# An attention and feed-forward kernel: a fixed order on every engine, weighted sums one step later, band scores with alternating heads

## The chip, the cores and the metric

One core of a Trainium2 chip. The core has five engines with queues of their own: TensorE (PE; PEld is its weight load), VectorE (DVE), ScalarE (ACT), GpSimd (POOL) and SyncE (SP, which here only issues DMAs). The metric is the time of the program on the device, in microseconds; 4103.99 us is the median of three runs of the kernel before (4099.41 to 4113.84).

## The reference

The input x has the shape (2, 256, 128, 128): batch, time T, band FB, channel C. All numbers are 32-bit floats.

```
xt = _ln(x, ln_t_w, ln_t_b).transpose(0, 2, 1, 3)
x = x + _mha(xt, t_wi, t_bi, t_wo, t_bo, H_T, cm).transpose(0, 2, 1, 3)
xf = _ln(x, ln_f_w, ln_f_b)
x = x + _mha(xf, f_wi, f_bi, f_wo, f_bo, H_F, bm)
xn = _ln(x, ln_n_w, ln_n_b)
h = jax.nn.gelu(xn @ w1.T + b1, approximate=False)
x = x + (h @ w2.T + b2)
```

`_ln` normalizes over the channels. `_mha` is attention with four heads of 32 channels: first over the 256 times of each band with a causal mask `cm`, then over the 128 bands of each time with a mask `bm` that leaves the bands at a distance of at most 16. The feed-forward layer has 512 hidden channels.

## The kernel before

A check at the start (`fold`, which also folds the normalization's weights into the projections) picks the path without a row maximum; `BoundedPath` is the one that runs.

**Groups.** The work is cut into 384 groups of 4 tiles, each of 128 rows by 128 channels. The first 128 are `OverTime` groups (two bands with 256 times each); a time group reads x, and its result goes to a buffer x1 in device memory. Then come 32 blocks, each of four `OverBands` groups (four times with 128 bands each) and four `FeedForward` groups on the same 16 times. I call the first 128 groups the time phase and the rest the band phase.

**Steps of a group.** Mean and variance (tiles stats, mv; DVE) and the power -1/2 (rstd; POOL); normalized rows (xh; DVE); transposed on TensorE (xp) and copied (xnT; DVE). Then, for attention, products for queries, keys and values (qp, kp, vp; TensorE), taken out of PSUM as qT (ACT), kT and v (DVE). The scores sp (TensorE) are split in two halves, `first_half` and `second_half`: in the time phase one of the group's two bands, in the band phase two of the four heads. Their exponentials go to p (ACT; its tiles are named pt in the time phase and pf in the band phase), and POOL sets the masked ones to 0 with affine selects. `weigh` makes the weighted sums op and the row sums rp of the exponentials (TensorE), `invert` the logarithm ln and from it the reciprocal r0 (ACT), `divide` the products t and u and the quotient oT, a Newton step (DVE). `output` makes the last product yp (TensorE) and adds it to rd or x2, into which POOL's `bias` has put the input plus a row (DVE); in the time phase rd is then stored. A feed-forward group has hidden products hp (TensorE), gelus hT (ACT), the output product zp (TensorE), which is added to res (DVE), and a store.

**Which part of the array.** A head has 32 channels. The score products of a head use 32 rows of TensorE's array (32*128 in the profile), the products op and rp of a head 32 columns (128*32).

**What sets the order.** `run` (lines 804 to 830) goes through the groups; in step n it calls steps of the groups n - 1 to n + 5 in the order of its list. What it writes is a priority: a scheduler with a timeline of its own then moves instructions of each engine past each other where it expects an engine to wait. Only the order of table loads on ACT is tied (`exp_set`, `gelu_set`, `load_exp_set`): Exp and Ln need one table set, Gelu another. PSUM has 8 banks, which the products take in turn; a product waits until the readers of the bank's last tile are done. p, hT have 2 buffers, rd has 4, the x tiles 3.

Lines that the prediction speaks of: 446 to 451 statistics, 457 xh, 467 xp, 469 xnT, 498 bias, 510 to 526 projections, 532 ln, 534 r0, 540 to 544 division, 550 yp, 579 and 582 scores of the time phase, 586 and 589 their exponentials and masks, 620 and 622 row sums there, 642 scores of the band phase, 644 and 648 exponentials and masks there, 667 and 670 weighted sums and row sums there, 689 hp, 709 zp, 766 load of x.

Of the kernel before, what the change touches and what calls it, by code (L numbers as in the profile page):

```python
# [18 lines left out]
P = 128  # L19
# [404 lines left out]
class Group:  # L424
# [3 lines left out]

    def __init__(self, path, src, dst, before=None, store=None):
        self.path, self.src, self.dst = path, src, dst  # L430
        self.before, self.store = before, store
# [9 lines left out]
    def statistics(self):  # L441
        path, nc = self.path, self.path.nc
        self.mv = path.small.tile([P, NT, 2], F32, name="mv")
        stats = path.small.tile([P, NT, 6], F32, name="stats")
        for i in range(NT):
            nc.vector.bn_stats(stats[:, i, :], self.src()[:, i, :])
        for i in range(NT):
            nc.vector.bn_aggr(self.mv[:, i, :], stats[:, i, :])  # L448
        self.rstd = path.small.tile([P, NT], F32, name="rstd")
        nc.gpsimd.tensor_scalar(self.rstd, self.mv[:, :, 1], EPS, None, ALU.add)  # L450
        nc.gpsimd.tensor_tensor(self.rstd, self.rstd, path.k.mhalf, ALU.pow)  # L451

    def normalize(self):
        path, nc = self.path, self.path.nc
        self.xh = path.work.tile([P, NT, P], F32, name="xh")
        for i in range(NT):
            nc.vector.tensor_scalar(
# [4 lines left out]
    def transpose(self):  # L462

        path, nc = self.path, self.path.nc
        xp = path.bank([P, NT * P], "xp")
        for i in range(NT):
            nc.tensor.transpose(xp[:, i * P : (i + 1) * P], self.xh[:, i, :], path.k.ident)  # L467
        self.xnT = path.work.tile([P, NT * P], F32, name="xnT")
        nc.vector.tensor_copy(self.xnT, xp)  # L469

    def first_half(self):
        pass
# [4 lines left out]
    def second_half(self):  # L477
        pass
# [3 lines left out]

    def weigh(self):
        pass
# [6 lines left out]


class Attention(Group):
    which = None

    def bias(self):
        self.dst_tile()
        self.path.nc.gpsimd.tensor_tensor(  # L498
            self.dst(), self.src(),
            self.path.k.orow[self.which].unsqueeze(1).to_broadcast([P, NT, P]), ALU.add,  # L500
# [5 lines left out]
    def queries_keys(self):  # L506
        path, nc = self.path, self.path.nc
        wf = path.k.wf[self.which]
        qp = path.bank([P, NT * P], "qp")
        nc.tensor.matmul(qp, wf[:, 0:P], self.xnT, start=True, stop=True)  # L510
        self.qT = path.work.tile([P, NT * P], F32, name="qT")
        nc.scalar.activation(self.qT, qp, AF.Identity, bias=path.k.bq[self.which], scale=1.0)

        kp = path.bank([P, NT * P], "kp")
        nc.tensor.matmul(kp, wf[:, P : 2 * P], self.xnT, start=True, stop=True)  # L515
        self.kT = path.work.tile([P, NT * P], F32, name="kT")
        nc.vector.tensor_copy(self.kT, kp)

    def values(self):
        path, nc = self.path, self.path.nc  # L520
        wv = path.k.wf[self.which][:, 2 * P : 3 * P]
        vp = path.bank([P, NT, P], "vp")
        for i in range(NT):
            nc.tensor.matmul(vp[:, i], self.xnT[:, i * P : (i + 1) * P], wv, start=True, stop=True)  # L524
        self.v = path.work.tile([P, NT, P], F32, name="v")
        nc.vector.tensor_copy(self.v, vp)

    def invert(self):

        path, nc = self.path, self.path.nc  # L530
        ln = path.work.tile([P, NT * P], F32, name="ln", bufs=2)
        path.exp_set(nc.scalar.activation(ln, self.rp, AF.Ln))  # L532
        self.r0 = path.work.tile([P, NT * P], F32, name="r0", bufs=2)
        path.exp_set(nc.scalar.activation(self.r0, ln, AF.Exp, scale=-1.0))  # L534

    def divide(self):

        path, nc = self.path, self.path.nc
        t = path.work.tile([P, NT * P], F32, name="t", bufs=2)
        nc.vector.tensor_tensor(t, self.rp, self.r0, ALU.mult)  # L540
        u = path.work.tile([P, NT * P], F32, name="u", bufs=2)
        nc.vector.tensor_tensor(u, self.op, self.r0, ALU.mult)  # L542
        self.oT = path.work.tile([P, NT * P], F32, name="oT", bufs=2)
        nc.vector.scalar_tensor_tensor(self.oT, t, 2.0, u, ALU.subtract, ALU.mult)  # L544

    def output(self):
        path, nc = self.path, self.path.nc
        yp = path.bank([P, NT, P], "yp")
        for i in range(NT):
            nc.tensor.matmul(  # L550
                yp[:, i], self.oT[:, i * P : (i + 1) * P], path.k.wn[self.which], start=True, stop=True
            )
        nc.vector.tensor_tensor(self.dst(), yp, self.dst(), ALU.add)
# [8 lines left out]
class OverTime(Attention):  # L562
# [6 lines left out]
    def dst_tile(self):  # L569
        rd = self.path.work.tile([P, NT, P], F32, name="rd", bufs=4)  # L570
        self.dst = lambda: rd

    def scores(self, s):
        path, nc = self.path, self.path.nc
        W, a = self.W, 2 * s * P
        for h in range(H):
            r = rows_of(h)
            sp = path.bank([P, W], "sp")
            nc.tensor.matmul(
                sp[:, 0 : 2 * P], self.kT[r, a : a + P], self.qT[r, a : a + 2 * P], start=True, stop=True  # L580
            )
            nc.tensor.matmul(  # L582
                sp[:, 2 * P : W], self.kT[r, a + P : a + 2 * P], self.qT[r, a + P : a + 2 * P],
                start=True, stop=True,
            )
            path.exp_set(nc.scalar.activation(self.p[:, s, h, :], sp, AF.Exp))  # L586
        for n in (0, 2):
            blk = self.p[:, s, :, n * P : (n + 1) * P]
            nc.gpsimd.affine_select(  # L589
                out=blk, in_=blk, compare_op=ALU.is_ge, fill=0.0, base=0,  # L590
# [3 lines left out]
    def first_half(self):  # L594
        self.p = self.path.work.tile([P, 2, H, self.W], F32, name="pt", tag="p", bufs=2)
        self.scores(0)

    def second_half(self):
        self.scores(1)

    def weigh(self):
        path, nc = self.path, self.path.nc
        p, v, W = self.p, self.v, self.W
        op = path.bank([P, 2, 2 * P], "op")
        for s in range(2):
            for h in range(H):
                r = rows_of(h)
                nc.tensor.matmul(
                    op[r, s, :], v[:, 2 * s, r], p[:, s, h, 0 : 2 * P], start=True, stop=False
                )  # L610
            for h in range(H):
                r = rows_of(h)
                nc.tensor.matmul(
                    op[r, s, P : 2 * P], v[:, 2 * s + 1, r], p[:, s, h, 2 * P : W],
                    start=False, stop=True,
# [284 lines left out]
```

## Time and profile before

| | |
|---|---|
| median of three runs | 4103.99 us (4099.41 to 4113.84) |
| the profiled execution's own time | 4108.16 us |
| its span, first to last instruction | 4106.3 us |
| busy: TensorE, DVE, POOL, ACT | 3682.2, 2327.0, 1909.9, 1595.4 us |
| mean granted clock of TensorE | 0.953 |
| DMA | 140.52 MB, 34 GB/s over the span |

A row of the groups or of the waits names line, engine and tile; "yp L550 <- DVE oT L544" is the product yp in line 550 waiting for DVE's tile oT from line 544, with the total, the number and the longest of these waits. In the timeline stand start, length, engine, line, tiles out<-in, and the number of instructions merged; a length of many TensorE records is from the start of the first to the modelled end of the last, so successive rows overlap, and the distance of two starts says what the first costs. A matmul of 32-bit floats is two records.

### The profile page before, as it was taken

The page shows a single profiled execution, that of the slowest core. Times are in us where ns is not written, and L with a number is a line of the kernel's source. Part 1 is how long each engine was busy: PE and PEld are TensorE (multiplying, and loading weights), DVE is VectorE, ACT ScalarE, POOL GpSimd, SP SyncE. Part 2 cuts the span into 40 slices and gives each one's busy share as a digit, 9 for nine tenths or more (in the row PEclk, how much of TensorE's full clock was granted, in tenths as well). Part 3 has the DMA queues.
Part 4 walks back from the last instruction along what each step waited for, and adds up shares of the span by engine and source line. Part 5 has one row for each costly group of instructions (what it writes and reads, how often), then busy time and mean ns, then how long its engine had stood idle before and what let it go on. Part 6 is the DMA issues. An engine that isn't in the chain of part 4 may idle for free.

```text
span 4106.3 us, 77158 instructions
## 1 busy us (share of the span) xinstructions
PE 3682.2 (90%) x31270; PEld 2508.3 (61%) x31270; DVE 2327.0 (57%) x6702; ACT 1595.4 (39%) x2880; POOL 1909.9 (47%) x2182
## 2 busy tenths in 40 slices
PE   6998998888988998899998998899889998999988
PEld 4555555555555566666666666666666665666666
DVE  6666666666665555554555555555555555555553
ACT  3444444444444433333333333333333333333333
POOL 4454454454545444444544444444444454444442
PEclk9999999999999999999999999999999999999999
DMA  2112111121121100010000100010001100010000
GB/s 75 47 46 57 45 48 55 48 55 48 45 56 46 55 24 21 22 38 26 22 21 24 37 24 21 21 40 24 22 21 30 34 21 21 24 39 21 11 14 20
DMA packets 222861, 140.52 MB, mean 34 GB/s; under 512 B 7968, under 2 KB 205984, under 8 KB 222496
## 3 DMA queue, kind: packets, MB, share of 16 engines
q1 hardware_dynamic: 221248, 134.45, 11.7%
q8 instruction: 248, 4.06, 0.4%
q10 hardware_dynamic: 1248, 1.05, 0.1%
q14 instruction: 117, 0.96, 0.1%
HBM read 68.36 MB, written 67.11 MB: 33 GB/s over the span
## 4 chain that ended last, share of the span: by engine, by line
PE 56%; DVE 5%; ACT 3%; POOL 1%; issue 1%; ACTq 0%; POOLq 0%; DVEq 0%
PE zp L709 11%; PE hp L689 11%; PE sp L642 7%; PE rp L670 6%; PE op L667 4%; PE xp L467 4%; PE yp L550 4%; PE vp L524 3%; PE qp L510 3%; PE kp L515 3%; DVE oT L544 2%; DVE t L540 1%; POOL pf L648 1%; DVE u L542 1%; ACT r L534 1%; ACT ln L532 1%
## 5 line engine op out<-in xcount | busy, mean ns | idle before, releaser
L648 POOL TENSOR_SCALAR_AFFINE_SELECT pf<-pf 128x1024 f32<-128x1024 f32 x512 | 595.8, 1167 | 889.8 <-ACT pf L644 875.7
L532 ACT ACTIVATE ln<-rp 128x512 f32<-128x512 f32 x256 | 152.9, 597 | 1516.6 <-PE rp L670 907.2
L550 PE MATMUL yp<-wn,oT 128*128 128x128 f32 x2048 | 333.1, 312 | 357.4 <-DVE oT L544 357.4
L469 DVE COPY xnT<-xp 128x512 f32<-128x512 f32 x384 | 264.4, 689 | 547.7 <-PE xp L467 547.7
L550 PEld LDWEIGHTS yp<-wn,oT 128*128 128x128 f32 x2048 | 282.5, 214 | 424.1 <-issue 248.8
L709 PEld LDWEIGHTS zp<-w2T_sb,hT 128*128 128x128 f32 x4096 | 474.8, 192 | 49.6 <-issue 38.5
L691 ACT ACTIVATE hT<-hp,b 128x512 f32<-128x512 f32 x512 | 341.4, 687 | 386.0 <-PE hp L689 382.0
L589 POOL TENSOR_SCALAR_AFFINE_SELECT pt<-pt 128x512 f32<-128x512 f32 x512 | 350.8, 705 | 301.4 <-ACT pt L586 301.2
L689 PE MATMUL hp<-xnT,w1f 128*128 128x512 f32 x1024 | 485.3, 605 | 0.0
L709 PE MATMUL zp<-w2T_sb,hT 128*128 128x128 f32 x4096 | 481.1, 276 | 0.0
L586 ACT ACTIVATE pt<-sp 128x384 f32<-128x384 f32 x1024 | 420.1, 495 | 127.2 <-PE sp L582 126.8
L642 PEld LDWEIGHTS sp<-qT,kT 32*128 32x128 f32 x4096 | 375.3, 186 | 107.6 <-issue 43.9
L644 ACT ACTIVATE pf<-sp 128x512 f32<-128x512 f32 x512 | 282.9, 596 | 371.3 <-PE sp L642 370.4
L642 PE MATMUL sp<-qT,kT 32*128 32x128 f32 x4096 | 420.4, 283 | 0.0
L451 POOL TENSOR_TENSOR rstd<-rstd,mhalf 128x4 f32<-128x4 f32 x384 | 403.8, 1057 | 23.6
L498 POOL TENSOR_TENSOR rd<-xt,orow 128x512 f32<-128x512 f32 x128 | 163.0, 1275 | 399.7 <-DMA x<-rd 336.5
L467 PEld LDWEIGHTS xp<-ident,xh 128*128 128x128 f32 x1536 | 176.8, 145 | 271.9 <-issue 219.3
L524 PE MATMUL vp<-wf,xnT 128*128 128x128 f32 x2048 | 312.9, 304 | 0.0
L713 DVE TENSOR_TENSOR res<-zp,res 128x512 f32<-128x512 f32 x128 | 88.2, 689 | 380.4 <-PE zp L709 380.4
L450 POOL TENSOR_SCALAR rstd<-mv 128x4 f32<-128x4 f32 x384 | 93.0, 247 | 441.3 <-DVE mv L448 441.3
L540 DVE TENSOR_TENSOR t<-rp,r 128x512 f32<-128x512 f32 x256 | 176.1, 688 | 213.9 <-ACT r L534 211.2
L670 PE MATMUL rp<-pf,ones 128*32 128x512 f32 x1024 | 296.7, 661 | 0.0
(97 smaller groups left out, 5808.5 us busy)
## 6 DMA issues: line engine op xcount, KB each, us to landing
xt<-in_x SPq DMA_DIRECT2D x64, 512.0 KB, 5.4
x<-rd SPq DMA_DIRECT2D x256, 128.0 KB, 1.9
out<-res SPq DMA_DIRECT2D x128, 256.0 KB, 2.3
xb<-x SPq DMA_DIRECT2D x32, 0.5 KB, 6.1
w1T_sb<-in_w1T ACTq DMA_DIRECT2D x1, 256.0 KB, 3.8
w2T_sb<-in_w2T ACTq DMA_DIRECT2D x1, 256.0 KB, 4.2
t_wiT_sb<-in_t_wiT ACTq DMA_DIRECT2D x1, 192.0 KB, 2.5
f_wiT_sb<-in_f_wiT ACTq DMA_DIRECT2D x1, 192.0 KB, 4.3
```

Of the source, the lines that this page charges most:

```text
L451: nc.gpsimd.tensor_tensor(self.rstd, self.rstd, path.k.mhalf, ALU.pow)
L467: nc.tensor.transpose(xp[:, i * P : (i + 1) * P], self.xh[:, i, :], path.k.ident)
L524: nc.tensor.matmul(vp[:, i], self.xnT[:, i * P : (i + 1) * P], wv, start=True, stop=True)
L550: nc.tensor.matmul(yp[:, i], self.oT[:, i * P : (i + 1) * P], path.k.wn[self.which], start=True, stop=True)
L586: path.exp_set(nc.scalar.activation(self.p[:, s, h, :], sp, AF.Exp))
L589: nc.gpsimd.affine_select(out=blk, in_=blk, compare_op=ALU.is_ge, fill=0.0, base=0, pattern=[[0, H], [1, P]], channel_multiplier=-1,)
L642: nc.tensor.matmul(sp[:, c], self.kT[r, c], self.qT[r, c], start=True, stop=True)
L648: nc.gpsimd.affine_select(out=blk, in_=blk, compare_op=ALU.is_ge, fill=0.0, base=BAND, pattern=[[0, len(heads)], [0, NT], [-s, P]], channe ...
L670: nc.tensor.matmul(self.rp[rows_of(h), :], path.k.ones[:, 0:D], self.p[:, h].rearrange("p i q -> p (i q)"), start=True, stop=True,)
L689: nc.tensor.matmul(hp, path.k.w1f[:, j * P : (j + 1) * P], self.xnT, start=True, stop=True)
L691: nc.scalar.activation(self.hT[:, j, :], hp, AF.Gelu, bias=path.k.b1[:, j : j + 1], scale=1.0)
L709: nc.tensor.matmul(zp[:, i], self.hT[:, j, i * P : (i + 1) * P], path.k.w2T[:, j, :], start=(j == 0), stop=(j == NI - 1),)
```

## The change

- **Order.** Every instruction of TensorE, DVE, ACT and POOL of this path goes through `InOrder`, which ties it to the place in which the program writes it. SP's DMAs are still placed by the scheduler. Issue and reading out of PSUM are methods of their own now (`take_transposed`, `take_query`, `take_key`, `take_values`, `first_function`, `second_function`, `finish`), so that `run` can place them apart.
- **A step later.** In step n the first score half of group n comes first, then `weigh`, `invert` and `divide` of group n - 1, then the second half. Before, `weigh` of group n stood at the end of step n. A feed-forward group's zp, its addition and its store are now its `weigh` and `divide`, and so are one step behind its gelus too. `weigh` makes the row sums ahead of the weighted sums. The load is called 7 groups ahead instead of 5, and `bias` in the group's own step instead of one before.
- **Band scores.** The two heads of a half alternate tile by tile. In the time phase the four first products of a half stand ahead of the four second ones.
- **Masks.** In the band phase POOL masks heads 0 to 2 one by one; head 3 is multiplied on DVE by a band of ones that is made at the start.
- **Other engines.** v in both phases, and kT in the band phase, are copied by ACT.
- **Buffers.** p and hT have 3 buffers, rd has 5. Banks are still 8.
- **Feed-forward groups** are normalized and transposed one group ahead (`AHEAD = 1`), attention groups two.

The core of the diff (a method's other lines only change `nc.vector` to `path.vector` and the like):

```diff
     def scores(self, s):
...
+        self.sp = [path.bank([P, W], "sp") for h in range(H)]
         for h in range(H):
             r = rows_of(h)
-            sp = path.bank([P, W], "sp")
-            nc.tensor.matmul(
-                sp[:, 0 : 2 * P], self.kT[r, a : a + P], self.qT[r, a : a + 2 * P], start=True, stop=True
-            )
...
+    def weights(self, s):
+        path = self.path
+        for h in range(H):
+            path.scalar.activation(self.p[:, s, h, :], self.sp[h], AF.Exp)
...
 class OverBands(Attention):
...
     def scores(self, heads):
-        path, nc = self.path, self.path.nc
+        path = self.path
+        self.sp = {h: path.bank([P, NT * P], "sp") for h in heads}
+        for i in range(NT):
+            c = slice(i * P, (i + 1) * P)
+            for h in heads:
+                r = rows_of(h)
+                path.tensor.matmul(self.sp[h][:, c], self.kT[r, c], self.qT[r, c], start=True, stop=True)
+
+    def weights(self, heads):
+        path = self.path
         for h in heads:
...
+            path.scalar.activation(self.p[:, h].rearrange("p i q -> p (i q)"), self.sp[h], AF.Exp)
+        for h in heads:
+            blk = self.p[:, h]
+            if h == H - 1:
+                path.vector.tensor_tensor(blk, blk, path.band.unsqueeze(1).to_broadcast([P, NT, P]), ALU.mult)
+                continue
+            for s in (1, -1):
+                path.gpsimd.affine_select(
+                    out=blk, in_=blk, compare_op=ALU.is_ge, fill=path.zero, base=BAND,
+                    pattern=[[0, NT], [-s, P]], channel_multiplier=s,
+                )
+
+    def take_key(self):
+        path = self.path
+        self.kT = path.work.tile([P, NT * P], F32, name="kT")
+        path.scalar.copy(self.kT, self.kp)
...
+class InOrder:
...
+        def pinned(*args, **kwargs):
+            return self.tc.keep_in_program_order(emit(*args, **kwargs))
...
-        self.load_exp_set()
-        for n in range(-5, len(groups) + 1):
...
-            do(n + 5, "load")
-            do(n + 1, "transpose", "bias")
-            do(n - 1, "divide")
-            do(n, "first_half")
-            do(n + 1, "queries_keys")
-            do(n, "second_half")
-            do(n + 2, "normalize")
-            do(n - 1, "output")
-            do(n + 1, "values")
-            do(n + 3, "statistics")
-            do(n, "weigh")
+        self.scalar.preload_act_table_set(EXP_SET)
+        for n in range(-7, len(groups) + 2):
+
+            turn = at(n, FeedForward) and at(n - 1, OverBands)
+            if at(n, OverBands) and at(n - 1, FeedForward):
+                self.scalar.preload_act_table_set(EXP_SET)
+            do(n + 7, "load")
+            near(n, 1, "statistics")
+            near(n, 0, "normalize")
+            do(n, "first_half")
+            if not turn:
+                do(n, "first_function")
+            do(n, "bias")
+            do(n - 1, "weigh", "invert", "divide")
+            if turn:
+                do(n, "first_function")
+            do(n, "second_half", "second_function")
+            do(n + 1, "queries_keys", "take_query", "take_key", "values", "take_values")
+            near(n, 0, "transpose")
+            near(n, 0, "take_transposed")
+            do(n - 1, "output", "finish")
```

`near(n, far, name)` calls the step for the group n + d + far if that group's `AHEAD` is d.

**DVE in the time phase, before**, around the division of one group (numbers after the names are buffers; the x tile xt_12540 is a new block of four groups):

```order
L540 TENSOR_TENSOR t_11808<-rp_11786,r0_11797 128x512
L542 TENSOR_TENSOR u_11810<-op_11769,r0_11797 128x512
L448 BN_AGGR mv_12746<-stats_12747 128x2 x4
L446 BN_STATS stats_12870<-xt_12540 128x6 x2
L446 BN_STATS stats_12993<-xt_12540 128x6 x2
L446 BN_STATS stats_13119<-xt_12540 128x6 x2
L446 BN_STATS stats_13242<-xt_12540 128x6 x2
L544 SCALAR_TENSOR_TENSOR oT_11812<-t_11808,u_11810 128x512
```

**And after**, one whole step:

```order
L796 BN_STATS stats_11413<-xt_10791 128x6 x4
L796 BN_AGGR mv_11412<-stats_11413 128x2 x4
L796 TENSOR_SCALAR xh_11425<-xt_10791,mv_11289,rstd_11299 128x128 x4
L796 TENSOR_TENSOR t_11481<-rp_11451,r0_11479 128x512
L796 TENSOR_TENSOR u_11483<-op_11460,r0_11479 128x512
L796 SCALAR_TENSOR_TENSOR oT_11485<-t_11481,u_11483 128x512
L796 COPY kT_11511<-kp_11507 128x512
L796 COPY xnT_11525<-xp_11520 128x512
L796 TENSOR_TENSOR rd_11326<-yp_11527,rd_11326 128x512
```

Before, half of the statistics of all four groups of a new block stand between u and oT of an old group; after, each step has the four of one group, ahead of its t. (In the changed kernel line 796, the call in `InOrder`, stands for all of them.)

**TensorE in the band phase, before**, a step of one band group:

```order
L667 MATMUL op_21695<-pf_21627,v_21572 32x128 x2
L670 MATMUL rp_21712<-pf_21627,ones_87 32x512 x2
L467 MATMUL xp_21721<-ident_76,xh_21664 128x128 x4
L642 MATMUL sp_21736<-qT_21644,kT_21648 128x128 x4
L642 MATMUL sp_21742<-qT_21644,kT_21648 128x128 x4
L510 MATMUL qp_21750<-xnT_21726,wf1_143 128x512
L515 MATMUL kp_21754<-xnT_21726,wf1_143 128x512
L667 MATMUL op_21695<-pf_21627,v_21572 32x128 x14
L670 MATMUL rp_21712<-pf_21627,ones_87 32x512 x2
```

**And after**, from the end of one step through the next one's first scores and its `weigh` of the group before:

```order
L796 MATMUL xp_17683<-ident_76,xh_17598 128x128 x4
L796 MATMUL yp_17690<-wn1_146,oT_17651 128x128 x4
L796 MATMUL sp_17710<-qT_17672,kT_17674 128x128
L796 MATMUL sp_17711<-qT_17672,kT_17674 128x128
...
L796 MATMUL rp_17727<-pf_17603,ones_87 32x512 x4
L796 MATMUL op_17732<-pf_17603,v_17586 32x128 x16
```

The four products of a head stood together and now alternate with the other head's (sp_17710 and sp_17711); rp came in two pairs of heads with other work between them, and now all four stand together, for a p whose exponentials were made a step before.

273 lines of the change are left out of this document (145 added, 128 removed).

## The prediction

> **What bounds the kernel now.** I read the page first (busy times, then the waits), next the list of waits, and then the timeline of TensorE in one stretch of each phase. "Time phase" is the attention over time (tiles pt, lines 573 to 627), "band phase" the blocks of four band groups and four feed-forward groups (pf, hT).
>
> ```profile
> PE 3682.2 (90%) x31270; PEld 2508.3 (61%) x31270; DVE 2327.0 (57%) x6702; ACT 1595.4 (39%) x2880; POOL 1909.9 (47%) x2182
> core 0: 4106.3 us, clock 0.953
> PE yp L550 <- DVE oT L544: 357.4, 223, 5.1
> DVE stats L446 <- DMA xt<-in_x: 61.1, 33, 5.1
> xt<-in_x SPq DMA_DIRECT2D x64, 512.0 KB, 5.4
> L586 ACT ACTIVATE pt<-sp x1024: 484/492/512, 44.3 to 1425.7; 128x384 f32<-128x384 f32 x171
> L589 POOL TENSOR_SCALAR_AFFINE_SELECT pt<-pt x512: 630/635/1110, 46.0 to 1426.9; 128x512 f32<-128x512 f32 x171
> L644 ACT ACTIVATE pf<-sp x512: 580/597/612, 1431.4 to 4057.7; 128x512 f32<-128x512 f32 x171
> ```
>
> TensorE is busy for 3682.2 of 4106.3 us; no other engine passes 57%. Of its 4106.3 - 3682.2 = 424.1 us of idling, 357.4 are one wait: the output product yp for the divided sums oT. And its clock averaged 0.953, so up to 0.047 x 4106.3 = 193 us went to half speed. The time phase lasts to about 1430, the band phase from there to the end.
>
> The timeline of TensorE, time phase (start, length, instructions, idle before in brackets):
>
> ```profile
> 988.72 1.16 PE L550 MATMUL yp<-wn,oT 128*128 128x128 f32 x8 [0.20 <-DVE oT L544]
> 989.71 1.06 PE L524 MATMUL vp<-wf,xnT 128*128 128x128 f32 x8
> ...
> 991.80 1.04 PE L620 MATMUL rp<-pt,ones 128*32 128x512 f32 x8
> ...
> 994.01 0.73 PE L579 MATMUL sp<-qT,kT 32*128 32x256 f32 x8
> 994.55 0.42 PE L582 MATMUL sp<-qT,kT 32*128 32x128 f32 x8
> 994.90 1.12 PE L510 MATMUL qp<-xnT,wf 128*128 128x512 f32 x2
> ...
> 997.97 1.16 PE L550 MATMUL yp<-wn,oT 128*128 128x128 f32 x8 [0.20 <-DVE oT L544]
> ...
> 1010.63 2.07 PE L550 MATMUL yp<-wn,oT 128*128 128x128 f32 x8 [3.61 <-DVE oT L544]
> ```
>
> One step without the wait is 997.97 - 988.72 - 0.20 = 9.05 us. The average is (1425.7 - 44.3)/127.5 = 10.8 us, because some steps end like the last row: 3.61 us of idling, after which yp takes 2.07 instead of 1.16 us.
>
> The same in the band phase, with one row of ScalarE:
>
> ```profile
> 2034.35 1.06 PE L524 MATMUL vp<-wf,xnT 128*128 128x128 f32 x8
> ...
> 2036.54 0.66 PE L467 MATMUL xp<-ident,xh 128*128 128x128 f32 x4
> 2037.12 1.71 PE L642 MATMUL sp<-qT,kT 32*128 32x128 f32 x16
> 2038.76 1.13 PE L510 MATMUL qp<-xnT,wf 128*128 128x512 f32 x2
> ...
> 2040.68 1.07 PE L667 MATMUL op<-pf,v 128*32 128x128 f32 x28
> 2041.57 1.03 PE L670 MATMUL rp<-pf,ones 128*32 128x512 f32 x4
> 2042.53 1.71 PE L642 MATMUL sp<-qT,kT 32*128 32x128 f32 x16
> 2046.73 1.13 PE L550 MATMUL yp<-wn,oT 128*128 128x128 f32 x8 [2.49 <-DVE oT L544]
> 2047.70 1.60 PE L524 MATMUL vp<-wf,xnT 128*128 128x128 f32 x8
> ...
> 2051.51 0.44 PE L467 MATMUL xp<-ident,xh 128*128 128x128 f32 x2
> ...
> 2053.85 0.60 ACT L532 ACTIVATE ln<-rp 128x512 f32<-128x512 f32 x1 [8.97 <-PE rp L670]
> 2054.10 2.82 PE L642 MATMUL sp<-qT,kT 32*128 32x128 f32 x32
> 2057.30 1.13 PE L550 MATMUL yp<-wn,oT 128*128 128x128 f32 x8 [0.39 <-DVE oT L544]
> 2059.33 0.41 PE L667 MATMUL op<-pf,v 128*32 128x128 f32 x4 [0.90 <-POOL pf L648]
> 2059.57 1.03 PE L670 MATMUL rp<-pf,ones 128*32 128x512 f32 x4
> ```
>
> From vp to the xp after it: 2036.54 - 2034.35 = 2.19 us at full rate, 2051.51 - 2047.70 = 3.81 us behind the 2.49 us wait. Such a wait costs 1.62 us more than itself. The 0.90 us wait before 2059.33 is followed by rp at its normal 1.03 us: no loss.
>
> **The change, term by term.**
>
> *Work of TensorE at full clock, before.* 3682.2 minus the clock's loss. Part of the 193 us lies in the idling itself; I take 175 (150 to 193): 3507 us.
>
> *Heads alternate in the band scores.* A pass of two heads is 16 records. The run of 32 records takes 2.82, one of 16 takes 1.71, so each further head adds (2.82 - 1.71)/2 = 0.555 and one head alone would take 1.71 - 0.555 = 1.155. If two heads run side by side, a pass costs about one head: 0.555 less, and 2 passes x 128 groups x 0.555 = 142 us. Ends: nothing (alternating could hinder the weight loads), and half of the 2038.76 - 2037.12 = 1.64 us pass, 0.82 x 256 = 210 us. I take 142: in the time phase four heads need 994.90 - 994.01 = 0.89 us for all their columns, so heads do run side by side there.
>
> There the change also writes the four 256-column products ahead of the four 128-column ones. I count nothing for it: before has them head by head, and still the eight 256-column records start (994.01 on) ahead of the eight 128-column ones (994.55 on), with 0.89 us in all. The Trainium skill (TensorE: Matmul & The Clock Gate, Part 3: Packing small matmuls) says that matmuls start and end strictly in program order. By that rule four heads written one after the other would take up to 4 x 0.89 us a pass, and up to 2.67 x 256 = 680 us would be there to gain; the trace differs, with 0.89 us.
>
> *Row sums of four heads at once.* Before, the band phase runs rp as two pairs of heads (x4), each 2042.53 - 2041.57 = 0.96 us, because the masks of a pair come first. Now all four stand together, as in the time phase, where eight records take 1.04 against 1.03 for four. So 0.96 x 128 = 123 us go. Ends: 100 to 130.
>
> *The waits.* In the time phase the 33 waits for the load, about one for each of 32 loads, fall where DVE has eight of the 16 stats of a new block ahead of an oT: yp and everything behind it on TensorE then waits. After, each step starts with its own four stats and the load is issued four steps ahead of them instead of two: 36 us against 5.4 us to land. On SP it passes stores whose sums are two or three steps old; it waits for a bias two steps old, so nothing is held behind it. What is late next? From ln to yp takes 2057.30 - 2053.85 = 3.45 us. ln now stands behind the step's first exponentials: in the time phase about 1.0 + 4 x 0.492 = 3.0 us after the step begins, so yp can start at 6.45; TensorE comes to it at 9.05 - 0.99 = 8.06 us. Slack 1.6 us: no wait. In the band phase ln stands at 1.1 + 2 x 0.597 + 0.1 = 2.4, yp could start at 5.85, and TensorE arrives about 1.7 us later, as q, k, v and xp stand between. Not so at three places of a block:
>
> - last band group: no q, k, v follow. Scores 1.1, rp 0.96, op about 1.05 (28 of 32 records take 0.89), scores 1.1, xp 0.5: TensorE is at yp at 4.7 and waits 1.15. Then the first hp waits about 0.45 for xnT, which on DVE now stands behind oT and the mask.
> - first feed-forward group: yp of the last band group, 3.45 us behind an ln that has only the second hp pair and xp (about 2.2) and the ln's own delay in front: 0.55.
> - second and third: hp follows directly on its own xp; between lie a copy of 512 columns and two handovers, 0.69 + 0.26 = 0.95, and half of it, 0.5, in the third, where a second xp stands between.
>
> The sum is 3.6 us, x 32 blocks = 115 us. The price of the copy is this row, with the others of the moved work:
>
> ```profile
> L469 DVE COPY xnT<-xp 128x512 f32<-128x512 f32 x384 | 264.4, 689 | 547.7 <-PE xp L467 547.7
> L526 DVE COPY v<-vp 128x512 f32<-128x512 f32 x256 | 175.9, 687 | 51.6 <-PE vp L524 33.2
> L512 ACT ACTIVATE qT<-qp,bq 128x512 f32<-128x512 f32 x256 | 179.1, 699 | 71.1 <-PE qp L510 71.1
> L544 DVE SCALAR_TENSOR_TENSOR oT<-t,u 128x512 f32<-128x512 f32 x256 | 200.6, 783 | 4.6
> L451 POOL TENSOR_TENSOR rstd<-rstd,mhalf 128x4 f32<-128x4 f32 x384 | 403.8, 1057 | 23.6
> L498 POOL TENSOR_TENSOR x<-xb,orow 128x512 f32<-128x512 f32 x128 | 158.2, 1267 | 7.0 <-DMA xb<-x 4.7
> ```
>
> *Half speed after the new waits.* Only the 1.15 us one is long enough to matter; 0.90 cost nothing and 2.49 cost 1.62. Half of the 32 blocks at 1.62: 26 us (0 to 52). The Trainium skill (TensorE: Matmul & The Clock Gate, Why this matters for your kernels) asks only that gaps stay under about 3 us. By that the 26 us would be 0 and the time 3394; the trace differs, since the 2.49 us gap above has already halved the rate.
>
> *Counted at nothing.* v and, in bands, kT go to ScalarE: 0.6 to 0.7 us each (between the exponential of 512 columns and qT), 384 of them, 265 us on an engine 39% busy; they lie beside TensorE's xp and yp. The mask of one head on DVE has no row; between v's 0.687 and oT's 0.783 us, it lies beside TensorE's q and k, and if that cover were gone it would cost 0.7 x 128 = 90 us. The 24 instead of 16 selects per four groups, of half the size, take 6 x 0.635 = 3.8 us of POOL per band step. The later bias, the deeper buffers and the feed-forward products one step after their gelus shift work that is not waited for.
>
> *Start and end.* TensorE idles some 35 us before the first products; with the tail 37 us.
>
> Sum: 3507 - 142 - 123 + 37 + 115 + 26 = 3420 us of span. The profiled execution took 4108.16 against its span of 4106.3 and a median of 4103.99; these differences cancel to 2 us and I leave them.
>
> **The rivals.**
>
> *POOL becomes the bound of the band steps.* Six selects, the rstd pair and the bias: at 0.635 us 3.8 + 1.06 + 1.27 = 6.1 of a step of 8.6 us. It decides from (8.6 - 2.3)/6 = 1.05 us a select. For it: the slowest select took 1.11. Against: the middle is 0.635. At 1.11 a step takes 9.0 plus the handovers between the queue's waits, about 0.7 more than forecast: 128 x 0.7 = 90 us, 3510. Chance 0.12.
>
> *Alternating brings no overlap* (so that the change doesn't do what it says): the 142 us stay, 3562. For: the heads of a pass have never stood so. Against: the four heads at 0.89 us. Chance 0.08.
>
> *Slower: the fixed place of yp makes TensorE wait in every attention step, and each wait halves the rate.* Price: 256 x (wait + 1.62). Against 3420 it reaches 4104 at (4104 - 3420)/256 = 2.7 us a step, a wait of 1.1 us; for that the chain from ln to yp would have to take 1.6 + 1.1 more than its 3.45 us. At a wait of 1.6 us it gives 3420 + 824 = 4244. For it: 223 waits at just this place now, and a scheduler can fill such a hole where a fixed order can't. Against: the step of delay, which puts 1.6 us of other work in front. Chance 0.03.
>
> **How the numbers follow.** Forecast 3420 with chance 0.76; 0.01 for no difference. Low end: if the waits are half as long (-57), no half speed (-26) and the scores gain a little more (-35), 3300. High end: the second rival (3562) with unforeseen waits of 0.1 us in each of 384 steps, 3600. 0.3% (12 us) is about what a measurement of this kernel can tell from no change: faster 0.96, same 0.01, slower 0.03.
>
> **What would show it.** Right: the wait of yp for oT falls from 357 to under 60 us, all of it in the band phase; xp to hp waits appear at about 1 us; a pass of two heads takes about 1.15 busy; a time step is 9 us throughout; the clock is over 0.98. Wrong: TensorE busy well above 3300 us at full clock; waits for pf from POOL in each band step; yp waiting in time steps.

## The result, and the profile after

The changed kernel takes 3305.18 us (median of four runs, 3304.38 to 3305.64) against 4101.7 us for the kernel before in the same rounds (4098.27 to 4113.84): a ratio of 0.8054, 95% interval 0.8036 to 0.8071. The forecast was 3420 us, range 3300 to 3600: right in direction and in most of its terms, 115 us too slow, and with the measured time only 5 us above the low end of the range. The profiled execution has a span of 3302.9 us.

From the page, the clocks, the waits of TensorE and the tiles pt and pf of the changed kernel (all its operations stand in line 796):

```profile
PE 3183.9 (96%) x31270; PEld 2259.0 (68%) x31270; DVE 2191.5 (66%) x6446; ACT 1803.8 (55%) x3264; POOL 1843.4 (56%) x2441
core 0: 3302.9 us, clock 0.999
PE hp L796 <- DVE xnT L796: 52.9, 96, 0.8
PE yp L796 <- DVE oT L796: 43.1, 64, 1.0
L796 ACT ACTIVATE pt<-sp x1024: 483/497/561, 34.5 to 1127.4; 128x384 f32<-128x384 f32 x171
L796 ACT ACTIVATE pf<-sp x512: 589/596/604, 1131.6 to 3258.7; 128x512 f32<-128x512 f32 x171
```

TensorE was busy 90% of a longer span and is now busy 96%, at full clock. The 357 us of waiting for oT are 43, and 53 us of waiting for xnT are new. The time phase (pt) fell from 1381 to 1093 us, the band phase (pf) from 2626 to 2127.

One whole time step of TensorE:

```profile
803.80 0.94 PE L796 MATMUL sp<-qT,kT 32*128 32x256 f32 x16
804.66 1.50 PE L796 MATMUL rp<-pt,ones 128*32 128x512 f32 x16
805.98 1.48 PE L796 MATMUL op<-pt,v 128*32 128x256 f32 x32
807.39 0.94 PE L796 MATMUL sp<-qT,kT 32*128 32x256 f32 x16
808.26 1.12 PE L796 MATMUL qp<-xnT,wf 128*128 128x512 f32 x2
809.22 1.02 PE L796 MATMUL kp<-xnT,wf 128*128 128x512 f32 x2
810.08 1.05 PE L796 MATMUL vp<-wf,xnT 128*128 128x128 f32 x8
810.97 0.60 PE L796 MATMUL xp<-ident,xh 128*128 128x128 f32 x4
811.41 1.06 PE L796 MATMUL yp<-wn,oT 128*128 128x128 f32 x8
812.39 0.94 PE L796 MATMUL sp<-qT,kT 32*128 32x256 f32 x16
```

No row has an idle time in brackets; a step takes 812.39 - 803.80 = 8.59 us.

The last two band steps of a block, and the turn to its feed-forward groups:

```profile
1756.69 1.16 PE L796 MATMUL sp<-qT,kT 32*128 32x128 f32 x16
1757.78 1.07 PE L796 MATMUL rp<-pf,ones 128*32 128x512 f32 x8
...
1759.65 1.16 PE L796 MATMUL sp<-qT,kT 32*128 32x128 f32 x16
...
1765.53 1.23 PE L796 MATMUL rp<-pf,ones 128*32 128x512 f32 x6
...
1767.99 1.16 PE L796 MATMUL sp<-qT,kT 32*128 32x128 f32 x16
...
1770.72 1.13 PE L796 MATMUL yp<-wn,oT 128*128 128x128 f32 x8 [0.97 <-DVE oT L796]
1772.35 1.96 PE L796 MATMUL hp<-xnT,w1f 128*128 128x512 f32 x4 [0.51 <-DVE xnT L796]
```

A pass of two heads costs 1757.78 - 1756.69 = 1.09 us. The sums after it cost 1759.65 - 1757.78 = 1.87 us, but in the last band step 1767.99 - 1765.53 = 2.46: 0.59 us that no row of TensorE calls a wait. The weight loads do: there rp stands for GpSimd's mask of the group before.

```profile
1766.14 0.11 PEld L796 LDWEIGHTS rp<-pf,ones 128*32 128x32 f32 x2 [0.46 <-POOL pf L796]
```

### The profile page after: what moved, and what is told of

Its sections match the earlier page's. It is cut to its first block, busy times and chain, and to the rows that moved or that the text cites. A ratio compares the mean times of both kernels' runs of the same rounds, so it can differ in the third digit from the quotient of the medians.

```text
span 3302.9 us, 77870 instructions
## 1 busy us (share of the span) xinstructions
PE 3183.9 (96%) x31270; PEld 2259.0 (68%) x31270; DVE 2191.5 (66%) x6446; ACT 1803.8 (55%) x3264; POOL 1843.4 (56%) x2441
## 3 DMA queue, kind: packets, MB, share of 16 engines
q10 hardware_dynamic: 1248, 1.05, 0.1%
## 4 chain that ended last, share of the span: by engine, by line
PE 89%; DVE 7%; ACT 2%; issue 1%; DMA 0%; POOL 0%; SPq 0%; ACTq 0%; DVEq 0%
PE sp L796 14%; PE zp L796 14%; PE hp L796 12%; PE rp L796 10%; PE qp L796 8%; PE vp L796 7%; PE op L796 7%; PE kp L796 7%; PE yp L796 6%; PE xp L796 4%; DVE xnT L796 2%; DVE oT L796 1%; DVE t L796 1%; ACT r L796 1%; DVE u L796 1%; ACT ln L796 1%
## 5 line engine op out<-in xcount | busy, mean ns | idle before, releaser
L796 POOL TENSOR_SCALAR_AFFINE_SELECT pf<-pf 128x512 f32<-128x512 f32 x768 | 545.3, 718 | 100.3 <-ACT pf L796 74.1
L796 PE MATMUL hp<-xnT,w1f 128*128 128x512 f32 x1024 | 493.9, 605 | 52.9 <-DVE xnT L796 52.9
L796 PE MATMUL sp<-qT,kT 32*128 32x128 f32 (+1 forms) x8192 | 536.2, 315 | 0.0
L796 PEld LDWEIGHTS sp<-qT,kT 32*128 32x128 f32 x8192 | 433.2, 185 | 87.6 <-issue 55.1
L796 PEld LDWEIGHTS vp<-wf,xnT 128*128 128x128 f32 x2048 | 269.7, 192 | 123.0 <-issue 92.2
L796 POOL TENSOR_SCALAR_AFFINE_SELECT pt<-pt 128x512 f32<-128x512 f32 x512 | 314.0, 637 | 58.5 <-ACT pt L796 58.4
L796 PE MATMUL yp<-wn,oT 128*128 128x128 f32 x2048 | 275.1, 277 | 43.1 <-DVE oT L796 43.1
L796 PEld LDWEIGHTS hp<-xnT,w1f 128*128 128x128 f32 x1024 | 174.2, 190 | 202.0 <-issue 131.3
L796 PE MATMUL qp<-xnT,wf 128*128 128x512 f32 x512 | 285.8, 640 | 0.8 <-DVE xnT L796 0.8
L796 DVE SCALAR_TENSOR_TENSOR oT<-t,u 128x512 f32<-128x512 f32 x256 | 272.9, 1066 | 8.9
L796 PE MATMUL vp<-wf,xnT 128*128 128x128 f32 x2048 | 270.5, 275 | 0.0
```

The costliest lines, as they stand in the source:

```text
L796: return self.tc.keep_in_program_order(emit(*args, **kwargs))
```

## The experiments

My theory: delay and fixed order together take the waits away; two heads side by side and four row sums at once make TensorE's own work shorter. Rivals: the parts bring nothing by themselves, or GpSimd is the next bound. Times are medians; "more" and "less" are against the changed kernel's 3305.2 us, ratios against the kernel before.

**Heads one after the other again.**

```diff
-        for i in range(NT):
-            for h in heads:
+        for h in heads:
+            for i in range(NT):
```

> The changed kernel with one thing undone: the two heads of a band-score pass stand one behind the other again. My theory: side by side a pass of two heads costs TensorE what one head costs, and in turn 0.555 us more; TensorE is the bound in every step, so 256 x 0.555 = 142 us come back: 3305 + 142 = 3447 us (3425 to 3465), with a pass at 1.71 us in the timeline. Rival: TensorE takes up the other head's products ahead by itself wherever it can, and the written order gives nothing: 3305 us within 12.

Measured: 3410.6 us (ratio 0.8317, 0.8299 to 0.8336), 105 more. The score products of this run, then those of the changed kernel, in the groups of TensorE:

```profile
L796 PE MATMUL sp<-qT,kT 32*128 32x128 f32 (+1 forms) x8192 | 676.4, 315 | 0.0
```

```profile
L796 PE MATMUL sp<-qT,kT 32*128 32x128 f32 (+1 forms) x8192 | 536.2, 315 | 0.0
```

Their busy time differs by 140.2 us: the term of 142 is shown. Only 105 of it are in the time, because the slower scores cover other things: the waits for oT fell from 43.1 to 27.8 us, and with longer steps the masks are ready, so that the last band step's sums take 1.87 us too (32 x 0.59 = 19 us).

**The sums in the same step as their exponentials, order still fixed.**

```diff
-            do(n - 1, "weigh", "invert", "divide")
...
             do(n - 1, "output", "finish")
+            do(n, "weigh", "invert", "divide")
```

> The changed kernel with the delay undone: weigh, invert and divide of group n stand at the end of step n, behind the products of the next group, in a fixed order as before this edit. My theory: TensorE then waits in every step for the exponentials and masks just made. Time steps: scores, projections, transposes and yp take about 6.1 us, the second mask is done at about 6.9: 0.8 us of wait. Band steps: 6.6 against 8.0 us: 1.4 us. Feed-forward steps: zp waits about 0.9 us for its own gelu. 128 x (0.8 + 1.4 + 0.9) = 400 us: 3700 us (3550 to 3850). Rival: the delay matters little, since a fixed order with alternating heads is what gained the time: under 3365 us.

Measured: 3983.6 us (0.9715, 0.9693 to 0.9736), 678 more, beyond what I expected. Its waits:

```profile
PE rp L796 <- POOL pf L796: 222.6, 241, 1.5
PE rp L796 <- POOL pt L796: 153.6, 128, 1.4
```

Now TensorE stands in every attention step for the mask of the exponentials it has just caused: 376 us. Another 125 us, which I did not expect, are 128 waits of xp for xh. Without the delay all the rest of the change is worth 118 us, not 796.

**The order of TensorE, DVE and GpSimd left to the scheduler, ACT's fixed.**

```diff
-        self.tensor, self.vector = InOrder(tc, tc.nc.tensor), InOrder(tc, tc.nc.vector)
-        self.scalar, self.gpsimd = InOrder(tc, tc.nc.scalar), InOrder(tc, tc.nc.gpsimd)
+        self.tensor, self.vector = tc.nc.tensor, tc.nc.vector
+        self.scalar, self.gpsimd = InOrder(tc, tc.nc.scalar), tc.nc.gpsimd
```

> The changed kernel's program with TensorE, DVE and POOL given back to the scheduler; only ACT keeps the written order. My theory: the fixed order is worth what the waits of yp cost, since the scheduler moves statistics and transposes ahead of the division; alternating heads may be pulled apart again. 3450 to 3800 us, with yp waiting for oT for over 150 us. Rival: the written program with its delay is what counts and the scheduler finds the same order: 3305 us within 30.

Measured: 3910.6 us (0.9534, 0.9511 to 0.9557), 605 more, clock 0.943. The waits for oT are back, in the band phase, and one for kT joins them in the time phase, about one for each load. The heads of a pass still alternate. The two waits:

```profile
PE yp L585 <- DVE oT L579: 231.1, 96, 3.3
PE sp L616 <- DVE kT L549: 169.8, 30, 7.5
```

Neither part makes do without the other: undone alone, each gives back more than three quarters of the gain.

**The kernel before with its load called earlier.**

```diff
-        for n in range(-5, len(groups) + 1):
+        for n in range(-7, len(groups) + 1):
...
-            do(n + 5, "load")
+            do(n + 7, "load")
```

> The kernel before with one edit: the load is called 7 groups ahead instead of 5. My theory: the long waits of yp in the time phase (about one in four steps) come from eight statistics that stand on DVE between u and oT and wait for the load. With an earlier load 61 us of DVE's wait go and part of the half speed behind them, while the statistics themselves (8 x 0.2 us) still stand there: 4102 - 60 to - 160, 3940 to 4040 us. Rival: the division is late in any case because the row sums come late in the step, and the load is a bystander: 4102 us within 12.

Measured: 4102.2 us (1.0002, 0.9987 to 1.0017): no change. But it doesn't test the load, since that still landed late (DVE's waits of stats for xt: 59.4 us, 61.1 before). There are three x buffers; the load waits for the last reader of an old one, GpSimd's bias, wherever it is called. So:

**The kernel before with five x buffers, load called 9 ahead.**

```diff
-        self.xpool = ctx.enter_context(tc.tile_pool(name="xpool", bufs=3))
+        self.xpool = ctx.enter_context(tc.tile_pool(name="xpool", bufs=5))
...
-            do(n + 5, "load")
+            do(n + 9, "load")
```

> The kernel before with five x buffers instead of three and its load called 9 groups ahead instead of 5; nothing else. Theory of the prediction, as far as it names the late load: a load that lands earlier lets the scheduler place the statistics of a block where DVE waits for nothing, the waits of stats for x (61 us) and about 33 waits of yp of 3.6 us in the time phase go, with 1 us each of half speed: 3930 to 4010. Rival, the eight statistics stand ahead of an oT wherever the load lands, so that the order on DVE makes the wait and not the load: stats wait less but yp still 300 to 360 us, 4080 to 4115.

Measured: 3934.0 us (0.9589, 0.9572 to 0.9607), 167 less than the kernel before. The waits of TensorE in the time phase, first of before, then of this run, and the exponentials of this run:

```profile
PE yp L550 <- DVE oT L544: 135.1, 126, 5.1
```

```profile
PE yp L550 <- DVE oT L544: 37.6, 126, 0.8
L586 ACT ACTIVATE pt<-sp x1024: 484/493/512, 44.1 to 1271.4; 128x384 f32<-128x384 f32 x171
```

The waits fall by 97.5 us and the time phase by 1381.4 - 1227.3 = 154; the 57 us between go mostly to the rate behind each wait (granted clock of the phase 0.94 before, 0.99 here). But the edit changes two things, as the theory said it would: the load lands in time, and the scheduler places the statistics elsewhere. DVE in a time step of this run:

```profile
995.14 0.68 DVE L544 SCALAR_TENSOR_TENSOR oT<-t,u 128x512 f32<-128x512 f32 x1
995.74 0.86 DVE L446 BATCH_NORM_STATS2 stats<-xt 128x6 f32<-128x128 f32 x4
```

The statistics stand behind oT, four at a time; between u and oT of a time step, where the profile before has eight of them 28 times, there are none. That more buffers and an earlier call remove the long waits is shown; which part of it is the landing itself and which the new order on DVE, no run separates.

**All masks on GpSimd.**

```diff
-            if h == H - 1:
+            if h == H:
```

> The changed kernel with the mask of head 3 back on GpSimd, so 8 selects per band step instead of 6. Theory that GpSimd is the next bound of the band steps: at 0.718 us a select (the changed kernel's mean) a step has 8 x 0.718 + 1.28 + 1.49 = 8.5 us of GpSimd against steps of 8.2 and 7.75 us, the rp of the third band step already waits some 0.6 us for a mask of a step before, and this grows by up to 1.4 us a step: 2 to 4 us a block, 60 to 130 us in all, 3365 to 3435, with waits of rp for GpSimd's pf of at least 60 us in the profile. Rival, GpSimd has slack (its busy share is 56%) and DVE is relieved: 3290 to 3317.

Measured: 3331.0 us (0.8121, 0.8107 to 0.8134), 26 more, less than I expected. In the waits of the weight loads, of this run and of the changed kernel:

```profile
PEld rp L796 <- POOL pf L796: 83.1, 96, 1.2
```

```profile
PEld rp L796 <- POOL pf L796: 39.1, 64, 0.8
```

The wait for masks is there already (two loads in each of 32 blocks) and grows with two more selects. GpSimd holds up single steps, not the block: the first sums of the next block don't wait. That it catches up in the feed-forward steps is my reading.

**The row sums in pairs of heads, one pair ahead of the weighted sums, one behind.**

```diff
-        for h in range(H):
+        sums((0, 1))
...
+        sums((2, 3))
```

> The changed kernel with the row sums of the band phase in two pairs of heads again, one ahead of the weighted sums and one behind. Theory that two pairs far apart cost one more pass of 0.96 us and that four heads side by side save it: 128 x 0.96 = 123 us, less up to 20 us that waits for masks and for oT give back, 3405 to 3430. Rival, the array takes the four heads one after the other in any case, or the pass lies in waits: 3305 to 3345.

Measured: 3540.7 us (0.8629, 0.8615 to 0.8644), 235 more: above both expectations. A band step, and the turn:

```profile
1824.09 0.62 PE L800 MATMUL rp<-pf,ones 128*32 128x512 f32 x2
...
1826.63 1.16 PE L800 MATMUL sp<-qT,kT 32*128 32x128 f32 x16
...
1840.14 2.05 PE L800 MATMUL yp<-wn,oT 128*128 128x128 f32 x8 [2.66 <-DVE oT L800]
1841.98 3.62 PE L800 MATMUL hp<-xnT,w1f 128*128 128x512 f32 x4
```

The sums take 1826.63 - 1824.09 = 2.54 instead of 1.87 us: 0.67 x 128 = 86 us directly. That is less than the 0.96 us a step of the theory. Most of the rest follows from it: ln now waits for the second pair, so yp waits 2.66 us at the turn (136.2 us in all instead of 43.1), and behind it yp and hp run at half the rate, 2.05 and 3.62 instead of 1.13 and 1.96. The clock falls to 0.970.

**xp ahead of the second half in every step** (`transpose` and `take_transposed` called ahead of `second_half`).

> The changed kernel with xp and its copy ahead of the second half of the scores in every step, so that the array changes its shape two times more in an attention step (32-column products, 128-column xp, 32-row scores, 128-column projections). Theory that each such change costs about 0.1 us of TensorE and that their smaller number is why a time step took 8.59 us and not 9.05: two more in 256 steps, 0.1 to 0.2 us a step, 25 to 50 us more, less the up to 36 us that the waits of hp give back: 3295 to 3320, with a time step of 8.7 to 8.8 us in the timeline. Rival, changes of shape cost nothing: a time step of 8.59 us and 3265 to 3275.

Measured: 3269.7 us (0.7972, 0.7959 to 0.7986), 35.5 less. The total is what the rival said, the step what the theory said:

```profile
791.84 0.94 PE L796 MATMUL sp<-qT,kT 32*128 32x256 f32 x16
...
795.43 0.66 PE L796 MATMUL xp<-ident,xh 128*128 128x128 f32 x4
796.02 0.94 PE L796 MATMUL sp<-qT,kT 32*128 32x256 f32 x16
...
800.58 0.94 PE L796 MATMUL sp<-qT,kT 32*128 32x256 f32 x16
```

A time step takes 800.58 - 791.84 = 8.74 us, 0.15 more, all of it at xp: 0.59 us to the next product, where it was 811.41 - 810.97 = 0.44. The array now goes from 32-column products to the full array and then to 32 rows, where it went from columns to rows directly: one change of shape more in a step, not two as I had written. It costs 0.15 us, some 20 us over the time phase; the gain is in the feed-forward steps, where no wait of hp is left. That is the next run by itself.

**xp ahead of the second half in feed-forward steps alone** (the same two calls, moved there only).

> The changed kernel with the transposition xp and its copy xnT ahead of the second pair of hidden products in feed-forward steps (behind it before). Theory that the waits of hp for xnT (0.78 and 0.35 us in each of 32 blocks, and nothing else late behind them) are on the path: 3305 - 32 x 1.13 = 3269, and the 0.51 us wait of the first feed-forward step stays, since its xp is still in the last band step; the waits of hp fall from 52.9 to about 16 us. Rival, something that runs beside (gelus, xh on DVE) is late next: xp waits for xh, or hp for a bank, and the time stays at 3293 to 3317.

Measured: 3251.1 us (0.7927, 0.7914 to 0.7940), 54 less, where I expected 36. The waits and busy time of this run:

```profile
PE hp L796 <- DVE xnT L796: 16.3, 32, 0.5
PE 3165.4 (97%) x31270; PEld 2258.6 (70%) x31270; DVE 2170.7 (67%) x6446; ACT 1802.9 (55%) x3264; POOL 1845.2 (57%) x2441
```

The waits fall by 52.9 - 16.3 = 36.6 us, and TensorE's busy time by 18.5, nearly all of it in hp (20 us): the 64 waits that are gone had cost some 0.29 us each besides their length, at full clock.

**GpSimd's bias at the end of the step** (`do(n, "bias")` moved ahead of the output).

> The changed kernel with GpSimd's bias (1.3 to 1.5 us) at the end of the step, behind all masks, instead of between those of the first and second half. Theory that rp in the third band step of a block stands 0.6 us because the masks of the step before end late on GpSimd: that wait goes, 32 x 0.6 = 19 us, 3280 to 3290; the 0.60 us that its pass of rp and op takes longer than the 1.87 us of the other steps goes with it. Rival, the 0.6 us is something of the array and no wait, or the power of the next statistics is late behind the bias instead: 3300 to 3345.

Measured: 3323.9 us (0.8106, 0.8092 to 0.8119), 19 more. The turn:

```profile
1705.12 1.97 PE L796 MATMUL yp<-wn,oT 128*128 128x128 f32 x8 [1.37 <-DVE oT L796]
1706.89 2.32 PE L796 MATMUL hp<-xnT,w1f 128*128 128x512 f32 x3
...
1910.23 1.13 PE L796 MATMUL yp<-wn,oT 128*128 128x128 f32 x8 [1.38 <-DVE oT L796]
```

The sums take 1.87 us for all four band groups now, so the 0.59 us was a wait for masks. But TensorE comes to yp earlier and waits 1.37 instead of 0.97 us there, and in 22 of the 32 blocks the clock is halved for 3.4 us at this turn (in the first row yp takes 1.97 us instead of 1.13); in the other ten, as in the last row, the same wait leaves the rate as it is. The time lies in the rival's range, but for neither of its reasons. A wait taken away ahead of a longer one is not won.

**The band phase without GpSimd's selects.** Heads 0 to 2 stay unmasked there.

> The changed kernel without GpSimd's selects in the band phase, so that heads 0 to 2 stay without their mask there; head 3 is still masked on DVE. Theory that DVE's mask takes 1.108 us in the mean because its two operands and GpSimd's selects stand in each other's way: without the selects 0.69 to 0.78 us, and oT in the band phase at 0.69 throughout. Rival, the operation takes 1.1 us by itself. The time itself says little: 3280 to 3325, since the 0.6 us of the third band step goes but a longer wait of yp can take its place, as with the bias at the end of the step.

Measured: 3271.5 us (one run), under the 3280 that I gave as the least. DVE's mask in this run, and in the changed kernel:

```profile
L792 DVE TENSOR_TENSOR pf<-pf,band x128: 680/685/693, 1135.8 to 3226.7; 128x512 f32<-128x512 f32 x128
```

```profile
L796 DVE TENSOR_TENSOR pf<-pf,band x128: 894/1114/1121, 1136.4 to 3259.5; 128x512 f32<-128x512 f32 x128
```

Without the selects the operation takes 0.685 us; beside them 1.114. The two engines stand in each other's way. As expected, oT in the band phase takes 0.691 to 0.693 us without the selects; in the changed kernel it takes up to 1.424.

**Early transposition, and yp behind other work at the turn.** The addition of the last step's yp moves behind the first hidden products and the sums of the next step, for two steps a block. By an oversight of the edit, yp of the third band group is formed and added twice. The core of the edit:

```diff
+            if second:
+                do(n - 2, "output", "finish")
             do(n - 1, "weigh")
+            if turn:
+                do(n - 2, "output", "finish")
```

> The changed kernel with the early transposition in feed-forward steps and, around the turn from bands to feed-forward, the products yp one place later: that of the last step's group stands behind the first hidden products and the weighted sums of the next step, so that oT has them as cover, and the statistics of these two steps stand behind the addition. Theory that the waits of yp for oT (0.97 and 0.37 us a block) and the last wait of hp (0.51) are on the path and nothing else is late: 3251 - 32 x 1.85 = 3192, some 10 to 20 us less where the waits also slow what follows: 3170 to 3205, with yp waiting under 10 us. Rival, the later additions make the statistics and xh late instead, and waits of xp or hp for DVE take their place: 3230 to 3275.

Measured: 3249.3 us (0.7921, 0.7908 to 0.7934), about what the early transposition alone gives (3251.1).

```profile
1756.51 1.13 PE L796 MATMUL yp<-wn,oT 128*128 128x128 f32 x8 [0.81 <-DVE oT L796]
...
1759.81 1.16 PE L796 MATMUL yp<-wn,oT 128*128 128x128 f32 x8
```

The first of the two yp is the one too many: it stands where nothing covers it, waits 0.81 us and takes 1.13 itself. The one meant, at 1759.81, and that of the next step wait for nothing. So this run doesn't decide. By an estimate from these rows, the product too many costs its wait and the 1.06 us to the next start, 1.87 us a block and 60 us in all; 3249 - 60 would be near the theory's 3192, but what the edit brings without the second yp was not measured.

## Why the prediction was right, and where its sizes were off

**Alternating heads, -142.** Right: 140.2 us of busy time, of which 105 are in the time when this part alone is undone. The rival of no overlap (3562) is refuted.

**Row sums, -123.** The size is about right, the reason only in part. A step's op and rp took 0.24 + 0.96 + 0.89 + 0.96 = 3.05 us before by the rows of the prediction; now three steps of 1.87 and one of 2.46, 2.02 in the mean: 1.03 x 128 = 132 us. But splitting the sums into two pairs again brings back 0.67 us a step, 86 us; the other 46 come from what else changed around them, which no run takes apart.

**Waits, +115.** The five places are the ones forecast. In one block they are 0.97 and 0.51 (rows above), and in the feed-forward steps yp 0.37 and hp 0.78 and 0.35, where the prediction had 1.15, 0.45, 0.55, 0.95 and 0.5:

```profile
1711.22 1.13 PE L796 MATMUL yp<-wn,oT 128*128 128x128 f32 x8 [0.37 <-DVE oT L796]
1720.58 1.98 PE L796 MATMUL hp<-xnT,w1f 128*128 128x512 f32 x4 [0.78 <-DVE xnT L796]
1729.07 1.98 PE L796 MATMUL hp<-xnT,w1f 128*128 128x512 f32 x4 [0.35 <-DVE xnT L796]
```

That is 2.98 instead of 3.6 us a block, 20 us of the miss. In the time phase none is left, as forecast; that the late load lay behind them is shown only together with the order it brought about on DVE.

**Half speed, +26.** It did not come: the waits end at 0.97 us, and the clock stays at 0.999. The prediction made the loss depend on the length of the wait, and that is not enough. A wait of 1.37 us was followed by half speed in 22 of 32 blocks (bias last); a wait of 1.2 us in every time step was not (sums in the same step, granted clock 1.00 over the whole phase); and with five x buffers yp waits 3.50 us in each of the 32 blocks and takes its normal 1.13 us behind it. What else decides, no run shows. The Trainium skill (TensorE: Matmul & The Clock Gate, Why this matters for your kernels) allows gaps up to about 3 us; the gaps of 1.37 us with half speed behind them differ from that.

**The time step, 9.05.** This was the mis-sized step of the prediction, and the largest part of the miss: it kept TensorE's work of before for all that it did not name. The step is 8.59 us, (9.05 - 8.59) x 128 = 59 us less. The new order puts q, k, v, xp and yp next to each other, all with the full array; before they stood between 32-row and 32-column products, with two more changes of shape in a step. Putting xp back between two of those, one more change, costs 0.15 us a step; the rest I attribute to the other change and to what stands next to what (kp, now followed by vp, 0.86 us to the next start, before 0.95), which no run tested one by one.

**Counted at nothing.** The mask on DVE took 1.108 us in the mean, outside the bounds of 0.687 to 0.783, and oT 1.066 instead of 0.783; both were off the path but for yp's waits. GpSimd's mean select rose to 0.718 us, under the 1.05 at which that rival decides, yet the masks hold up one band step in four, 32 x 0.59 = 19 us that the prediction did not have. The slower rival needed waits of yp in every step; there are two in a block.

**Start and end, +37.** The profile has 3302.9 - 3183.9 = 119.0 us of idling, of which 96.0 are the waits of hp and yp; 23 are left for start and end. The prediction took TensorE to idle some 35 us before the first products; in the profile before it is busy for 17.5 of the first 44 us, with the folding of the weights and the first projections.

The sum by the page: the forecast had 3507 - 142 - 123 = 3242 us of work at full clock, and 3183.9 were measured, 58 less. With 26 of half speed, 115 - 96 = 19 of waits and 37 - 23 = 14 of start and end that makes the 117 us between 3420 and the span. The parts named for the work (59 for the time step, 9 for the sums, less 2 for the heads) come to 66; because the base of 3507 held an estimate of 25 us either way for the half speed of before, these 8 us are not settled.

That the range held is in part luck. Its low end was made of waits half as long, no half speed and scores that gain more. The waits came out a sixth shorter, the half speed stayed away, the scores gained no more, and the largest part of the miss, the time step, was not among these reasons.

## What to carry to other kernels

A fixed order pays when each instruction's inputs are a step old: fixed without the delay, or delayed without the fixed order, this kernel keeps less than a quarter of the gain. After such a change, look where the pattern turns (here between band and feed-forward groups): the remaining waits sit there, and moving one transposition was worth another 54 us. When an order is rewritten, count the changes between full and partial array use too, and check that a load called earlier has a free buffer to land in.

## What the runs showed of the hardware

**DVE and GpSimd block each other.** The quotient oT, whose two operands are both in SBUF, in the time step above, and GpSimd's bias beside it:

```profile
808.96 1.18 DVE L796 SCALAR_TENSOR_TENSOR oT<-t,u 128x512 f32<-128x512 f32 x1
```

```profile
808.32 1.27 POOL L796 TENSOR_TENSOR rd<-xt,orow 128x512 f32<-128x512 f32 x1
```

The bias ends at 809.59 and oT at 810.14, 0.55 us behind it, nearly as if it had begun only then; its shortest run is 0.691 us. The same mask takes 0.685 us without selects and 1.114 with them, and a select that meets one takes up to 1.166 us against a median of 0.636:

```profile
L796 POOL TENSOR_SCALAR_AFFINE_SELECT pf<-pf x768: 624/636/1166, 1133.6 to 3262.4; 128x512 f32<-128x512 f32 x192
```

The Trainium skill (SBUF — State Buffer, SBUF: two separate sides) says that the port pair the two share is an exclusive lock for the whole instruction; these rows agree. So work moved from GpSimd to DVE is not taken off GpSimd in full: its mean select takes 0.718 us with the mask of head 3 on DVE, and 0.659 with all masks on GpSimd.

**A wait of TensorE costs more than its length**, and not only through half speed: 64 waits under 0.8 us, 36.6 us in all, were worth 54 us, at a clock of 0.999 with them and 1.000 without.

**How closely two heads alternate decides how far their matmuls overlap**: 1.64 us for a pass with four products of a head in a row, 1.09 alternating one by one, for the same 16 records.
